# A pairwise bilinear product with operands laid out by the host and its result held transposed

## The chip, the cores and the metric

The kernel runs on one core of a Trainium2 chip. The metric is the device time of one execution in microseconds (us). TensorE does matrix products, VectorE the elementwise work out of PSUM, ScalarE copies, GpSimd and SyncE issue DMA transfers; 16 DMA engines move data between HBM and the core's SBUF. A PSUM bank holds 512 f32 values in each of 128 partitions, and there are eight banks. Work that the host does before and after the launch (transposing arrays) is not in the metric.

## The reference, cut to what matters

```python
# r_inputs: (1024, 32, 128) f32     batch b, field, d
# L0_rec_W: (496, 128, 128) f32     pair p, e, d
pairs = list(itertools.combinations(range(32), 2))   # (i, j) with i < j, by rising i
v_i = inputs[:, I_IDX, :]
v_j = inputs[:, J_IDX, :]
transformed = jnp.einsum('bpd,ped->bpe', v_i, W)
return transformed * v_j                             # (1024, 496, 128) f32
```

For each of the 496 pairs (i, j) of the 32 fields, field i of every batch row is multiplied by the pair's own 128 x 128 matrix, and the result elementwise by field j. The inputs have 16.8 MB (x) and 32.5 MB (w), the output has 260 MB.

## The kernel before, in words

Batch lies on the partitions: the 1024 rows are eight tiles of 128. `_chunks` cuts the pairs, in the reference's order, into 46 runs of at most 16 pairs with the same i and neighbouring j. The main loop (L122) goes over the chunks, and in each over the batch tiles. One product (L162, or L140 for chunks of at most four pairs) has a 128 x 128 block of x_i, transposed, as the stationary operand and up to four transposed matrices w_p side by side (512 columns) as the moving one. Two of them fill a PSUM tile `po` of two banks, of which there are three. VectorE multiplies the tile by the fields j of the batch tile (L169, L149), which lie side by side in `x_sb`, into an output tile `ot` (four buffers of 8 KB a partition), and SyncE stores it to HBM (L175). One row of such a store is n x 512 bytes long, where n is the number of pairs in the chunk.

TensorE needs the contracted dimension d on the partitions, but x and w come with batch and e there. So the kernel transposes both on TensorE, against an identity: each w_p (`transpose_w`, L86) and each 128 x 128 block of x_i (`transpose_x`, L93), into PSUM tiles `pt` (two), from which ScalarE copies them to SBUF (L87 into `wt`, L94 into `xt`). That is 496 transposes of w and 31 x 8 = 248 of x. `prepare(c + 1)` (L111) does this for the next chunk when the current one is halfway through its batch tiles, and issues the load of the chunk after that (L76). All loads are issued from GpSimd's queue. At the start come the first chunk's w, the fields 0 to 16 of x by batch tile (L103), the second chunk's w, and then the other fields (L106). x stays in SBUF for the whole run.

The order on each engine is that in which the program issues the instructions; waits between engines and for free buffers are put in by the tile framework.

Of the kernel before, what the change touches and what calls it, by code (L numbers as in the profile page):

```python
# [7 lines left out]

F32 = mybir.dt.float32
ALU = mybir.AluOpType  # L10

P = 128
BANK = 4  # 128-wide fp32 blocks in one PSUM bank
MAXC = 16  # pairs per chunk
MAXB = 8  # batch tiles


def _chunks(nf):
    """Runs of pairs (i, j0..j0+n-1) that share i; pair numbers run on in this order."""
    out = []  # L20
    p0 = 0
    for i in range(nf - 1):
        j0 = i + 1
        left = nf - 1 - i
        while left:
            if left > MAXC:
                n = min(MAXC, -(-left // (2 * BANK)) * BANK)
            else:
                n = left
            out.append((i, j0, p0, n))  # L30
            j0 += n
            p0 += n
            left -= n
    return out


@with_exitstack
def kernel(
    ctx: ExitStack,
    tc: tile.TileContext,  # L40
    x: bass.AP,
    w: bass.AP,
    out: bass.AP,
):
    """out[b, p, e] = (sum_d x[b, i(p), d] * w[p, e, d]) * x[b, j(p), e]

    Batch lies on partitions. For one i, the pairs (i, j) with j = i+1.. are
    contiguous in w, in out and, as fields j, in x, so one product of
    x_i^T (stationary) with up to four w_p^T side by side fills a PSUM bank,
    and its elementwise factor is a contiguous slice of x.  # L50
    """
    nc = tc.nc
    B, NF, D = x.shape
    NB = B // P
    assert NB == MAXB and D == P

    cpool = ctx.enter_context(tc.tile_pool(name="const", bufs=1))
    wpool = ctx.enter_context(tc.tile_pool(name="w", bufs=2))
    tpool = ctx.enter_context(tc.tile_pool(name="t", bufs=2))
    opool = ctx.enter_context(tc.tile_pool(name="o", bufs=4))  # L60
    ps_t = ctx.enter_context(tc.tile_pool(name="ps_t", bufs=2, space=bass.MemoryType.PSUM))
    ps_o = ctx.enter_context(tc.tile_pool(name="ps_o", bufs=3, space=bass.MemoryType.PSUM))

    ident = cpool.tile([P, P], F32, tag="ident", name="ident")
    make_identity(nc, ident)
    x_sb = cpool.tile([P, NB, NF, D], F32, tag="x", name="x_sb")

    x_v = x.rearrange("(b p) f d -> p b f d", p=P)
    out_v = out.rearrange("(b p) q e -> p b q e", p=P)

    chunks = _chunks(NF)

    def load_w(c):
        _, _, p0, n = chunks[c]
        t = wpool.tile([P, MAXC, D], F32, tag="wn", name=f"wn_{c}")
        nc.gpsimd.dma_start(out=t[:, :n, :], in_=w[p0 : p0 + n].rearrange("q e d -> e q d"))  # L76
        return t

    def transpose_w(c, wn):
        n = chunks[c][3]  # L80
        wt = tpool.tile([P, MAXC, D], F32, tag="wt", name=f"wt_{c}")
        for k in range(0, n, BANK):
            m = min(BANK, n - k)
            pt = ps_t.tile([P, BANK, P], F32, tag="pt", name=f"ptw_{c}_{k}")
            for r in range(m):
                nc.tensor.transpose(pt[:, r, :], wn[:, k + r, :], ident)  # L86
            nc.scalar.copy(wt[:, k : k + m, :], pt[:, :m, :])  # L87
        return wt

    def transpose_x(i, xt, b0, nb):  # L90
        pt = ps_t.tile([P, BANK, P], F32, tag="pt", name=f"ptx_{i}_{b0}")
        for r in range(nb):
            nc.tensor.transpose(pt[:, r, :], x_sb[:, b0 + r, i, :], ident)  # L93
        nc.scalar.copy(xt[:, b0 : b0 + nb, :], pt[:, :nb, :])  # L94

    def new_xt(i):
        return tpool.tile([P, NB, P], F32, tag="xt", name=f"xt_{i}")

    # The first chunk needs x only up to its last field: those come first.
    w_nat = {0: load_w(0)}  # L100
    f0 = chunks[0][1] + chunks[0][3]
    for b in range(NB):
        nc.gpsimd.dma_start(out=x_sb[:, b, :f0, :], in_=x_v[:, b, :f0, :])  # L103
    w_nat[1] = load_w(1)
    for b in range(NB):
        nc.gpsimd.dma_start(out=x_sb[:, b, f0:, :], in_=x_v[:, b, f0:, :])  # L106

    w_t = {0: transpose_w(0, w_nat.pop(0))}
    x_t = {0: new_xt(0)}

    def prepare(c):  # L111
        """Transposed operands of chunk c, made while chunk c-1 is at work."""
        if c + 1 < len(chunks):
            w_nat[c + 1] = load_w(c + 1)
        w_t[c] = transpose_w(c, w_nat.pop(c))
        i = chunks[c][0]
        if i not in x_t:
            x_t[i] = new_xt(i)
            for b0 in range(0, NB, BANK):
                transpose_x(i, x_t[i], b0, BANK)  # L120

    for c, (i, j0, p0, n) in enumerate(chunks):  # L122
        wt, xt = w_t.pop(c), x_t[i]
        # batch tiles per store, and per PSUM tile (two banks)
        nb = 1
        while nb * 2 * n <= MAXC and nb < NB:
            nb *= 2
        bpb = BANK // n if n <= BANK else 0
        for b0 in range(0, NB, nb):
            ot = opool.tile([P, MAXC * D], F32, tag="ot", name=f"ot_{c}_{b0}")  # L130
            o4 = ot[:, : nb * n * D].rearrange("p (b q e) -> p b q e", b=nb, q=n)
            if c == 0:
                for b in range(b0, b0 + nb):
                    transpose_x(i, xt, b, 1)
            if bpb:
                for s in range(0, nb, 2 * bpb):
                    po = ps_o.tile([P, 2, BANK * D], F32, tag="po", name=f"po_{c}_{b0}_{s}")
                    for k in range(2):
                        for r in range(bpb):
                            nc.tensor.matmul(  # L140
                                po[:, k, r * n * D : (r + 1) * n * D],
                                xt[:, b0 + s + k * bpb + r, :],
                                wt[:, :n, :],
                                start=True,
                                stop=True,
                            )
                    for k in range(2):
                        bo = s + k * bpb
                        nc.vector.tensor_tensor(  # L149
                            o4[:, bo : bo + bpb],  # L150
                            po[:, k, : bpb * n * D].rearrange("p (b q e) -> p b q e", b=bpb, q=n),
                            x_sb[:, b0 + bo : b0 + bo + bpb, j0 : j0 + n, :],
                            ALU.mult,
                        )
            else:
                for r in range(nb):
                    for k in range(0, n, 2 * BANK):
                        m = min(2 * BANK, n - k)
                        po = ps_o.tile([P, 2 * BANK, D], F32, tag="po", name=f"po_{c}_{b0}_{r}_{k}")
                        for h in range(0, m, BANK):  # L160
                            g = min(BANK, m - h)
                            nc.tensor.matmul(  # L162
                                po[:, h : h + g, :],
                                xt[:, b0 + r, :],
                                wt[:, k + h : k + h + g, :],
                                start=True,
                                stop=True,
                            )
                        nc.vector.tensor_tensor(  # L169
                            o4[:, r, k : k + m, :],  # L170
                            po[:, :m, :],
                            x_sb[:, b0 + r, j0 + k : j0 + k + m, :],
                            ALU.mult,
                        )
            nc.sync.dma_start(out=out_v[:, b0 : b0 + nb, p0 : p0 + n, :], in_=o4)  # L175
            half = (NB // 2) // nb * nb
            if b0 == half and c + 1 < len(chunks):
                prepare(c + 1)


_INS = ["r_inputs", "L0_rec_W"]
_OUT = ((1024, 496, 128), "float32")


# [17 lines left out]
```

## Time and profile before

| What | Value |
|---|---|
| Median of 3 runs | 979.3 us (979.02 to 979.58) |
| Profiled execution: span of its instructions (the page gives no other time for it) | 975.6 us |
| TensorE, products and transposes | busy 944.4 us, 97% |
| Weight loads (beside TensorE's products) | busy 483.9 us, 50% |
| VectorE | busy 611.5 us, 63% |
| ScalarE | busy 105.5 us, 11% |
| GpSimd | busy 55.8 us, 6% |
| HBM | read 49.28 MB, written 260.05 MB |
| DMA queue of SyncE (stores) | 65.9% of 16 engines' span |
| DMA queue of GpSimd (loads) | 16.0% of 16 engines' span |

The profile is that of one execution. Its lines name engines as PE (TensorE products), PEld (TensorE weight loads), DVE (VectorE), ACT (ScalarE), POOL (GpSimd) and SP (SyncE), and the source line after an L. A group of instructions is given with its count, its busy time, the mean ns of one, the idle time of the engine ahead of them and what ended it. A product of f32 operands stands in the counts as two passes. The ends of products are modelled, so that neighbouring ones overlap; their starts are measured.

### The profile page before, as it was taken

The page shows a single profiled execution, that of the slowest core. Times are in us where ns is not written, and L with a number is a line of the kernel's source. Part 1 is how long each engine was busy: PE and PEld are TensorE (multiplying, and loading weights), DVE is VectorE, ACT ScalarE, POOL GpSimd, SP SyncE. Part 2 cuts the span into 40 slices and gives each one's busy share as a digit, 9 for nine tenths or more (in the row PEclk, how much of TensorE's full clock was granted, in tenths as well). Part 3 has the DMA queues.
Part 4 walks back from the last instruction along what each step waited for, and adds up shares of the span by engine and source line. Part 5 has one row for each costly group of instructions (what it writes and reads, how often), then busy time and mean ns, then how long its engine had stood idle before and what let it go on. Part 6 is the DMA issues. An engine that isn't in the chain of part 4 may idle for free.

```text
span 975.6 us, 7916 instructions
## 1 busy us (share of the span) xinstructions
PE 944.4 (97%) x2920; PEld 483.9 (50%) x2920; DVE 611.5 (63%) x630; ACT 105.5 (11%) x205; POOL 55.8 (6%) x68
## 2 busy tenths in 40 slices
PE   6598999999999999999999999999999999999997
PEld 3244454544445454544545554455544555555565
DVE  2264666666666666666666666666666666666664
ACT  1101010000101010110101011011110011110111
POOL 3100000000000000000000000000000000000000
PEclk9798999999999999999999999999999999999999
DMA  8999777878787878787888878888887877777876
GB/s 334 424 422 368 306 311 324 326 299 342 296 339 303 327 294 339 308 320 297 328 321 310 319 307 300 327 314 320 339 295 317 313 312 303 305 296 283 303 294 219
DMA packets 63079, 309.85 MB, mean 318 GB/s; under 512 B 5953, under 2 KB 9025, under 8 KB 53825
## 3 DMA queue, kind: packets, MB, share of 16 engines
q1 hardware_dynamic: 52064, 260.07, 65.9%
q0 software_dynamic: 10976, 49.29, 16.0%
q8 instruction: 23, 0.38, 0.2%
q14 instruction: 16, 0.12, 0.0%
HBM read 49.28 MB, written 260.05 MB: 317 GB/s over the span
## 4 chain that ended last, share of the span: by engine, by line
PE 91%; DMA 7%; ACT 0%; POOL 0%; issue 0%; DVE 0%; DVEq 0%; POOLq 0%; ACTq 0%
PE po L162 81%; DMA wn<-in_L_rec_W_dram 7%; PE ptw L86 6%; PE ptx L93 3%; PE po L140 2%; DMA x_sb<-in_r_inputs_dram 1%; ACT wt L87 0%; POOL wn L76 0%; DVE ot L149 0%; DVEq L198 0%; ACT xt L94 0%; POOL ident masks.py:199 0%; POOL ident masks.py:197 0%; POOLq masks.py:199 0%; ACTq L87 0%
## 5 line engine op out<-in xcount | busy, mean ns | idle before, releaser
L162 PE MATMUL po<-wt,xt 128*128 128x512 f32 (+3 forms) x2112 | 853.8, 559 | 2.3 <-ACT xt L94 2.3
L169 DVE TENSOR_TENSOR ot<-po,x_sb 128x1024 f32<-128x1024 f32 (+3 forms) x608 | 598.4, 1008 | 350.3 <-PE po L162 344.8
L162 PEld LDWEIGHTS po<-wt,xt 128*128 128x128 f32 x2112 | 386.0, 190 | 407.7 <-issue 346.6
L87 ACT COPY wt<-ptw 128x512 f32<-128x512 f32 (+3 forms) x136 | 69.5, 550 | 822.8 <-PE ptw L86 822.8
L76 POOL DMA_DIRECT2D wn<-in_L_rec_W_dram x46 | 46.6, 1014 | 870.2 <-PE ptw L86 787.0
L86 PE MATMUL ptw<-ident,wn 128*128 128x128 f32 x496 | 71.8, 286 | 22.7 <-DMA wn<-in_L_rec_W_dram 22.7
L86 PEld LDWEIGHTS ptw<-ident,wn 128*128 128x128 f32 x496 | 62.2, 148 | 55.6 <-issue 28.7
L94 ACT COPY xt<-ptx 128x512 f32<-128x512 f32 (+1 forms) x68 | 35.9, 550 | 39.5 <-PE ptx L93 39.0
L93 PEld LDWEIGHTS ptx<-ident,x_sb 128*128 128x128 f32 x248 | 29.0, 141 | 16.4 <-ACT wt L87 9.7
L93 PE MATMUL ptx<-ident,x_sb 128*128 128x128 f32 x248 | 36.5, 276 | 0.5 <-ACT wt L87 0.4
L149 DVE TENSOR_TENSOR ot<-po,x_sb 128x512 f32<-128x512 f32 (+1 forms) x22 | 13.1, 638 | 9.6 <-PE po L140 9.6
L140 PE MATMUL po<-wt,xt 128*128 128x512 f32 (+3 forms) x64 | 18.2, 438 | 0.1
L140 PEld LDWEIGHTS po<-wt,xt 128*128 128x128 f32 x64 | 10.7, 190 | 6.3 <-issue 3.1
L106 POOL DMA_DIRECT2D x_sb<-in_r_inputs_dram x8 | 4.3, 533 | 27.5 <-DMA x_sb<-in_r_inputs_dram 21.2
L103 POOL DMA_DIRECT2D x_sb<-in_r_inputs_dram x8 | 4.3, 554 | 1.8 <-DMA wn<-in_L_rec_W_dram 1.8
L87 ACT ACT_TABLE_LOAD x1 | 1.3, 1283 | 0.7 <-PEq L190 0.7
masks.py:199 POOL TENSOR_SCALAR_AFFINE_SELECT ident<-ident 128x128 f32<-128x128 f32 x1 | 0.3, 305 | 0.1
masks.py:197 POOL MEMSET ident<- 128x128 f32 x1 | 0.2, 204 | 0.3 <-POOLq L190 0.3
L190 POOL MEMSET const-float32-0.0<- 128x1 f32 x1 | 0.1, 98 | 0.2 <-issue 0.2
L190 POOL MEMSET const-bfloat16-1.0<- 128x1 bf16 x1 | 0.1, 101 | 0.0
L190 POOL MEMSET const-uint8-127<- 128x1 uint8 x1 | 0.1, 101 | 0.0
L190 POOL MEMSET const-float32-1.0<- 128x1 f32 x1 | 0.1, 98 | 0.0
## 6 DMA issues: line engine op xcount, KB each, us to landing
out_dram<-ot SPq DMA_DIRECT2D x75, 1024.0 KB, 4.0
out_dram<-ot SPq DMA_DIRECT2D x98, 768.0 KB, 3.4
out_dram<-ot SPq DMA_DIRECT2D x24, 896.0 KB, 3.7
out_dram<-ot SPq DMA_DIRECT2D x32, 640.0 KB, 3.0
out_dram<-ot SPq DMA_DIRECT2D x24, 704.0 KB, 3.3
out_dram<-ot SPq DMA_DIRECT2D x16, 960.0 KB, 4.0
out_dram<-ot SPq DMA_DIRECT2D x24, 576.0 KB, 3.0
out_dram<-ot SPq DMA_DIRECT2D x16, 832.0 KB, 3.4
```

What stands on the lines that cost most here:

```text
L76: nc.gpsimd.dma_start(out=t[:, :n, :], in_=w[p0 : p0 + n].rearrange("q e d -> e q d"))
L86: nc.tensor.transpose(pt[:, r, :], wn[:, k + r, :], ident)
L87: nc.scalar.copy(wt[:, k : k + m, :], pt[:, :m, :])
L93: nc.tensor.transpose(pt[:, r, :], x_sb[:, b0 + r, i, :], ident)
L94: nc.scalar.copy(xt[:, b0 : b0 + nb, :], pt[:, :nb, :])
L103: nc.gpsimd.dma_start(out=x_sb[:, b, :f0, :], in_=x_v[:, b, :f0, :])
L106: nc.gpsimd.dma_start(out=x_sb[:, b, f0:, :], in_=x_v[:, b, f0:, :])
L140: nc.tensor.matmul(po[:, k, r * n * D : (r + 1) * n * D], xt[:, b0 + s + k * bpb + r, :], wt[:, :n, :], start=True, stop=True,)
L149: nc.vector.tensor_tensor(o4[:, bo : bo + bpb], po[:, k, : bpb * n * D].rearrange("p (b q e) -> p b q e", b=bpb, q=n), x_sb[:, b0 + bo : b ...
L162: nc.tensor.matmul(po[:, h : h + g, :], xt[:, b0 + r, :], wt[:, k + h : k + h + g, :], start=True, stop=True,)
L169: nc.vector.tensor_tensor(o4[:, r, k : k + m, :], po[:, :m, :], x_sb[:, b0 + r, j0 + k : j0 + k + m, :], ALU.mult,)
L190: nc = _bacc.Bacc("TRN2", target_bir_lowering=False, num_devices=1)
```

## The change

The host now hands over x as `xt` of shape (d, field, batch) and w as `wt` of shape (d, pair, e), with the pairs sorted by rising j (and by rising i within one j). It takes the output as (pair, e, batch) and turns it back after the launch.

On the chip, each pair has two products: the stationary operand is the pair's w with d on the partitions and e as its columns, the moving operand is x_i with d on the partitions and 512 batch rows as its columns. The result has e on the partitions and batch on the free dimension and fills a PSUM tile of two banks (four such tiles). VectorE multiplies the 1024 columns by x_j in the same layout (d and e have the same size and partition, so that one copy of x serves as both operands). Two pairs share an output tile of 1 MB (six buffers), and SyncE stores it in rows of 4 KB; the last two pairs are multiplied and stored by halves.

There are no transposes, no copies on ScalarE and no identity. w is loaded in chunks of eight pairs (512 KB, four buffers), issued from ScalarE's queue three chunks ahead. Each field of x is a tile of its own (512 KB); the fields 0 to 3 are issued from SyncE at the start, the fields 4 and 5 from ScalarE, and field j + 3 from ScalarE at the first pair with j.

The diff, cut to its core:

```diff
-def _chunks(nf):
-    """Runs of pairs (i, j0..j0+n-1) that share i; pair numbers run on in this order."""
...
+def _pairs():
+    return [(i, j) for j in range(1, NF) for i in range(j)]
...
-    def transpose_w(c, wn):
...
-                nc.tensor.transpose(pt[:, r, :], wn[:, k + r, :], ident)
-            nc.scalar.copy(wt[:, k : k + m, :], pt[:, :m, :])
...
-    def transpose_x(i, xt, b0, nb):
...
-    def prepare(c):
...
+    xpool = ctx.enter_context(tc.tile_pool(name="x", bufs=1))
+    wpool = ctx.enter_context(tc.tile_pool(name="w", bufs=4))
+    opool = ctx.enter_context(tc.tile_pool(name="o", bufs=6))
+    ppool = ctx.enter_context(tc.tile_pool(name="ps", bufs=4, space=bass.MemoryType.PSUM))
+
+    def load_x(f, eng, pieces=1):
+        x_sb[f] = xpool.tile([P, BT], F32, tag=f"x{f}", name=f"x_{f}")
+        s = BT // pieces
+        for k in range(pieces):
+            eng.dma_start(out=x_sb[f][:, k * s : (k + 1) * s], in_=xt[:, f, k * s : (k + 1) * s])
+
+    def load_w(c, splits=(0, WC)):
+        w_sb[c] = wpool.tile([P, WC, P], F32, tag="w", name=f"w_{c}")
+        for a, b in zip(splits, splits[1:]):
+            nc.scalar.dma_start(out=w_sb[c][:, a:b, :], in_=wt[:, c * WC + a : c * WC + b, :])
+
+    load_w(0, (0, 1, 3, WC))
+    load_x(0, nc.sync, 2)
+    load_x(1, nc.sync, 2)
+    load_x(2, nc.sync)
+    load_w(1)
+    load_x(3, nc.sync)
+    load_w(2)
+    load_x(4, nc.scalar)
+    load_x(5, nc.scalar)
+
+    out_v = out.rearrange("q e b -> e q b")
+    for q, (i, j) in enumerate(pairs):
+        if q % WC == 0 and q // WC + 3 < nchunk:
+            load_w(q // WC + 3)
+        if i == 0 and 5 < j + 3 < NF:
+            load_x(j + 3, nc.scalar)
+        po = ppool.tile([P, BT], F32, tag="po", name=f"po_{q}")
+        for h in range(0, BT, HB):
+            nc.tensor.matmul(
+                po[:, h : h + HB],
+                w_sb[q // WC][:, q % WC, :],
+                x_sb[i][:, h : h + HB],
+                start=True,
+                stop=True,
+            )
+        r = q % OC
+        if r == 0:
+            ot = opool.tile([P, OC, BT], F32, tag="ot", name=f"ot_{q}")
+        if q < NQ - OC:
+            nc.vector.tensor_tensor(ot[:, r, :], po[:, :], x_sb[j][:, :], ALU.mult)
+            if r == OC - 1:
+                nc.sync.dma_start(out=out_v[:, q - r : q + 1, :], in_=ot[:, :, :])
+        else:
+            for h in range(0, BT, HB):
+                s = slice(h, h + HB)
+                nc.vector.tensor_tensor(ot[:, r, s], po[:, s], x_sb[j][:, s], ALU.mult)
+                nc.sync.dma_start(out=out_v[:, q, s], in_=ot[:, r, s])
...
+    perm = _np.array([i * (2 * NF - 1 - i) // 2 + j - i - 1 for i, j in _pairs()])
+    xt = _np.ascontiguousarray(x.transpose(2, 1, 0))
+    wt = _np.ascontiguousarray(w[perm].transpose(2, 0, 1))
...
+    args.append(nc.dram_tensor("out_0_dram", (NQ, P, BT), F32, kind="ExternalOutput").ap())
...
+    y[:, perm, :] = got.transpose(2, 0, 1)
```

Here P = 128, NF = 32, NQ = 496, BT = 1024, HB = 512, WC = 8 and OC = 2.

More of the change, by code (lines that the diff above doesn't have):

```diff
@@ L5 @@
 from concourse import mybir
-from concourse.masks import make_identity
 from concourse._compat import with_exitstack
@@ L12 @@
 P = 128
-BANK = 4
-MAXC = 16
-MAXB = 8
-def _chunks(nf):
[L20 to L34, printed above, removed]
+NF = 32
+NQ = NF * (NF - 1) // 2
+BT = 1024
+HB = 512
+WC = 8
+OC = 2
+def _pairs():
+    return [(i, j) for j in range(1, NF) for i in range(j)]
 @with_exitstack
@@ L40 @@
     tc: tile.TileContext,
-    x: bass.AP,
-    w: bass.AP,
+    xt: bass.AP,
+    wt: bass.AP,
     out: bass.AP,
@@ L52 @@
     nc = tc.nc
[L53 to L77, printed above, removed]
@@ L79, in transpose_w @@
-    def transpose_w(c, wn):
[L80 to L88, printed above, removed]
-    def transpose_x(i, xt, b0, nb):
[L91 to L109, printed above, removed]
-    def prepare(c):
[L113 to L178, printed above, removed]
@@ L181 @@
-_INS = ["r_inputs", "L0_rec_W"]
-_OUT = ((1024, 496, 128), "float32")
+    pairs = _pairs()
+    xpool = ctx.enter_context(tc.tile_pool(name="x", bufs=1))
+    wpool = ctx.enter_context(tc.tile_pool(name="w", bufs=4))
+    opool = ctx.enter_context(tc.tile_pool(name="o", bufs=6))
+    ppool = ctx.enter_context(tc.tile_pool(name="ps", bufs=4, space=bass.MemoryType.PSUM))
+    x_sb = {}
+    def load_x(f, eng, pieces=1):
[3 more added lines that the diff above has]
+            eng.dma_start(out=x_sb[f][:, k * s : (k + 1) * s], in_=xt[:, f, k * s : (k + 1) * s])
@@ new lines @@
+    nchunk = NQ // WC
+    w_sb = {}
+    def load_w(c, splits=(0, WC)):
[11 more added lines that the diff above has]
+    load_x(5, nc.scalar)
@@ new lines @@
+    out_v = out.rearrange("q e b -> e q b")
+    ot = None
+    for q, (i, j) in enumerate(pairs):
[24 more added lines that the diff above has]
+                nc.sync.dma_start(out=out_v[:, q, s], in_=ot[:, r, s])
```

11 lines of the change are left out of this document (6 added, 5 removed).

## The prediction

> **What bounds the kernel now.** I read the page first: spans, busy times, slices, the chain that ended last and the costliest groups.
>
> ```profile
> span 975.6 us, 7916 instructions
> PE 944.4 (97%) x2920; PEld 483.9 (50%) x2920; DVE 611.5 (63%) x630; ACT 105.5 (11%) x205; POOL 55.8 (6%) x68
> ...
> HBM read 49.28 MB, written 260.05 MB: 317 GB/s over the span
> ...
> PE po L162 81%; DMA wn<-in_L_rec_W_dram 7%; PE ptw L86 6%; PE ptx L93 3%; PE po L140 2%; DMA x_sb<-in_r_inputs_dram 1%; ACT wt L87 0%; POOL wn L76 0%; DVE ot L149 0%; DVEq L198 0%; ACT xt L94 0%; POOL ident masks.py:199 0%; POOL ident masks.py:197 0%; POOLq masks.py:199 0%; ACTq L87 0%
> ```
>
> The reader is to see that TensorE is busy in 97% of the span and that the chain runs through its own work: the products (L162, L140), the transposes of w (L86) and of x (L93), and near the start through loads. VectorE is far from the bound. Memory traffic is 309.3 MB, and its rate comes next, from the view of windows (columns: TensorE, weight loads, VectorE, ScalarE, GpSimd busy, the granted clock, the DMA engines' busy share, GB/s).
>
> ```profile
> 0.00:24.00 24.00, 14.49 (x42) 7.74 (x43) 5.71 (x5) 4.33 (x8) 9.60 (x20) 1.00 0.87 332
> 24.00:48.00 24.00, 12.98 (x39) 6.57 (x38) 6.54 (x6) 3.22 (x8) 2.82 (x5) 0.79 1.01 424
> 48.00:73.00 25.00, 24.64 (x61) 11.22 (x60) 16.57 (x14) 0.27 (x1) 1.56 (x2) 1.00 1.01 422
> 73.00:98.00 25.00, 20.63 (x64) 11.31 (x63) 10.84 (x10) 3.39 (x6) 1.15 (x1) 0.86 0.96 371
> ...
> 400.00:600.00 200.00, 200.00 (x590) 98.82 (x589) 132.46 (x151) 18.00 (x34) 8.96 (x9) 1.00 0.81 314
> ...
> 910.00:922.70 12.70, 12.70 (x38) 6.33 (x37) 8.98 (x8) 1.30 (x4) 0.00 (x0) 1.00 0.86 318
> 948.00:955.00 7.00, 7.00 (x21) 3.26 (x20) 4.82 (x8) 0.00 (x0) 0.00 (x0) 1.00 0.52 199
> ...
> 950.00:976.00 26.00, 19.69 (x89) 12.90 (x88) 12.71 (x22) 4.58 (x9) 0.55 (x1) 0.98 0.63 224
> ```
>
> There are two regimes. Up to about 75 us the DMA engines are full (share 1.01, 424 GB/s) and TensorE has gaps. After 98 us TensorE has none (200.00 of 200.00 us) and the DMA engines follow at 0.81. So the main part is worth exactly what TensorE no longer has to do, as long as the DMA engines can follow the faster pace.
>
> **What one pair costs.** VectorE takes up each finished 1024-column PSUM tile as soon as it is there; in the timeline of a stretch without transposes (chunk i=15, 16 pairs) the starts therefore show TensorE's step.
>
> ```profile
> 709.62 1.22 DVE L169 TENSOR_TENSOR ot<-po,x_sb 128x1024 f32<-128x1024 f32 x1 [0.89 <-PE po L162]
> ...
> 725.07 1.22 DVE L169 TENSOR_TENSOR ot<-po,x_sb 128x1024 f32<-128x1024 f32 x1 [0.49 <-PE po L162]
> ```
>
> Nine steps lie between these two: (725.07 - 709.62) / 9 = 1.717 us for 1024 columns. That is two products of 512 columns, each recorded as two passes, so 0.429 us a pass. In the kernel before, 496 pairs times 8 batch tiles times 128 columns are 507,904 columns, or 496 such tiles. The changed kernel has 496 pairs times 1024 batch columns: the same 496 tiles. 496 x 1.717 = 851.6 us, before and after. Turning the product round (w stationary, x moving) changes no size: both operands stay 128 x 128 and 128 x 512 f32, and the weights are loaded once a pass in both.
>
> ```profile
> L162 PEld LDWEIGHTS po<-wt,xt 128*128 128x128 f32 x2112 | 386.0, 190 | 407.7 <-issue 346.6 <-DVE ot L169 40.4 <-ACT xt L94 5.6
> L169 DVE TENSOR_TENSOR ot<-po,x_sb 128x1024 f32<-128x1024 f32 x352 | 431.1, 1225 | 312.5 <-PE po L162 309.8 <-DMA out_dram<-ot 2.7
> ```
>
> A weight load of 190 ns lies beside a pass of 429 ns and stays hidden; uncovered, 1,984 of them would cost 377 us, but nothing in the change removes the cover. VectorE's multiply of 1024 columns keeps its form (PSUM and SBUF operand, both contiguous): 1.225 us against TensorE's 1.717 us, 496 x 1.225 = 608 us in all. It stays hidden, with 0.49 us to spare a pair, and four PSUM tiles of two banks instead of three let TensorE run a tile further ahead.
>
> **What is removed.** All 496 + 248 transposes, their copies on ScalarE, and the identity. The price of a warm transpose is read where a group of eight stands between two products in TensorE's timeline (the starts count, since the ends are modelled and overlap).
>
> ```profile
> 703.50 1.02 PE L162 MATMUL po<-wt,xt 128*128 128x512 f32 x2
> 704.36 1.04 PE L86 MATMUL ptw<-ident,wn 128*128 128x128 f32 x8
> 705.23 0.39 PE L162 MATMUL po<-wt,xt 128*128 128x128 f32 x2
> ```
>
> 705.23 - 704.36 = 0.87 us for eight, 0.109 us each; 744 x 0.109 = 81 us, all on the path. ScalarE's copies are off it and give nothing by themselves, but for those of the first chunk. The waits of TensorE, the start and the end:
>
> ```profile
> PE ptw L86 <- DMA wn<-in_L_rec_W_dram: 22.7, 3, 10.1
> PE po L162 <- ACT xt L94: 2.3, 6, 0.5
> ...
> 8.27 3.73 PE L86 MATMUL ptw<-ident,wn 128*128 128x128 f32 x16 [8.27 <-DMA wn<-in_L_rec_W_dram]
> ...
> 970.10 1.29 DVE L149 TENSOR_TENSOR ot<-po,x_sb 128x512 f32<-128x512 f32 x2 [2.04 <-PE po L140]
> ```
>
> The 22.7 us include the first 8.3 us; the idle time behind it stands in the windows, 25.3 us short of full up to 98 us (9.5 + 11.0 + 0.4 + 4.4). Account of before: 851.6 + 81 + 25.3 + 5.5 (from 970.1 to 975.6) = 963.4. The 12 us left are the stretches at a lower clock after waits and the first chunk, where single transposes, their copies and products alternate; they have no cause in the new kernel except at its start.
>
> **What is added.** *Start.* SyncE and ScalarE issue the loads at once, in the order of need. The first product needs 64 KB of w and 256 KB of x. Rows:
>
> ```profile
> out_dram<-ot SPq DMA_DIRECT2D x1, 512.0 KB, 3.2
> ...
> wn<-in_L_rec_W_dram POOLq DMA_DIRECT2D x1, 64.0 KB, 2.2
> ...
> SPq L190 <- PEq L190: 0.7, 1, 0.7
> ...
> L175 SPq DMA_DIRECT2D out_dram<-ot x310: 332/332/388, 17.8 to 971.4; - x155
> ```
>
> The queue is free at 0.7 us, an issue takes 0.33 us, and 256 KB that share the engines with the w pieces land in about 3 us, between the rows of 2.2 and 3.2: 4.0 us. Bounds: 3.0 (0.7 + 2.2) and the 8.3 us of before. *Cold clock.* After the wait that ends at 79.3 us the chain of waits shows two passes in twice the warm time:
>
> ```profile
> 81.29 1.71 PE po L162 x2
> ```
>
> 0.855 us a pass instead of 0.429. From 79.3 us, cold transposes and these passes fill some 4 us, so the new kernel, which begins cold, loses about half of 4 us: 2.0 (bounds 0 and 4, if an early wait makes it cold again). *Inputs in the first stage.* Pairs run by rising j, so field j is needed only at pair j(j-1)/2, and each load of a field is issued three j ahead. ScalarE's queue holds these loads behind those of w: the load of chunk c+3 waits until TensorE has ended chunk c-1, and a field's load may stand behind it. Field 8, the first so held, is issued when pair 7 has ended and needed at pair 28, some 35 us later, while the slowest loads below took 33.2 us with the engines full and sixteen of them (16.8 MB) queued:
>
> ```profile
> DMA to landing us min/median/max: 7.9/28.3/33.2
> ```
>
> I cost it at nothing. The load of w three chunks ahead has 24 pairs (41 us) of cover. If that cover goes, TensorE waits and VectorE and the stores behind it. *Stores.* SyncE's queue holds four fields' loads and then only stores of 1 MB, each waiting for VectorE's second multiply; nothing else is behind them. Their rows are 4 KB everywhere, where before they ran from 8 KB down to 0.5 KB with the width of the chunk. The worst moment is the sixteenth pair, near 5.8 + 16 x 1.717 = 33 us: 16 x 0.524 = 8.4 MB stored, five w chunks 2.6 MB, ten fields 5.2 MB, 16.2 MB in all, where 424 GB/s moves 13.7 MB in 32 us. The 2.5 MB that it is behind fit in the five 1 MB output tiles beside the one being filled. Cost nothing; below 340 GB/s it would stall VectorE. Later the need is 0.59 MB per 1.717 us, or 343 GB/s, and 309.3 MB / 859 us = 360 GB/s on average. What the DMA engines can do is the unknown that counts: full, they moved 424; in the other windows the rate at a full share is 314/0.81 = 388, 318/0.86 = 370, 199/0.52 = 383 and at the very end, with rows of 0.5 to 1.5 KB, 224/0.63 = 356. For rows of 4 KB I take 380 to 424, nearest to the 388 and 424 of wide chunks, so it is hidden. *End.* The last pair is multiplied and stored in halves: 0.65 us, an issue of 0.33 and a landing of about 3, with little queued ahead: 4.5 us, against 5.5 before (bounds 3.5 and 6).
>
> **The sum.** 4.0 + 2.0 + 851.6 + 4.5 = 862.1 us of span. The page gives a span and no separate time for the profiled execution; the median of the runs, 979.3, is 3.7 us above it, which I keep: 865.8, said as 865.5.
>
> **A rule weighed against the trace.** The windows show 424 GB/s for 24 us and 422 for 25. The Trainium skill, "DMA: Bandwidth & Descriptors", section "Where 436 GB/s comes from", says that for transfers between HBM and SBUF the HBM side binds at about 358 GB/s per core. By it the time would be an estimate of 309.3 / 0.358 = 864 us of transfers alone, about 875 in all. The trace goes against it in those windows; the skill's "HBM Reference", section "Specifications (TRN2)", itself allows about 425 for a core that streams alone.
>
> **The rivals.** *DMA engines become the bound.* The windows with 424 are full of reads of x; where stores dominate, no window shows more than 318, since nothing asked for more. If 4 KB stores run at the worst ratio, 356 GB/s, 309.3 MB take 869 us, with 1 us ahead and some 4 us behind, 874 of span, 878 in all. VectorE would wait for output tiles and TensorE for PSUM all along. Against it: 383 with rows of 2 KB (948 to 955 us). The skill's rule above, as a rival, is this one; its 875 lies at the same place. *The start slips.* A load of x or w comes late in the first 60 us as w did before: three waits of up to 10.1 us, 22.7 in all. One such wait with a cold restart, 10 + 2, gives 877; the small issue order above speaks against it. *Slower than before.* The stores collapse: one pair is now one contiguous 512 KB block, where the DMA engines had written rows far apart; if this order brings the mixed rate under 309.3 / 975 = 317 GB/s, the kernel is slower; at 300 GB/s it takes 1031 + 9 = 1040 us. For it, only that no row here shows that order; against it, that no row with busy engines converts to under 356. *The change doesn't do what it says*, because transposes were hidden beside something else: no, since TensorE had 200.00 of 200.00 us.
>
> **How the numbers follow.** Forecast 0.74; DMA bound 0.13; slip at the start 0.09; stores collapse 0.04. A measurement of this kernel tells some 0.2% (2 us) from no change; only the last case comes near, shared as 0.03 slower and 0.01 same. The forecast's own range is 860 to 870 (start, cold clock and end at their bounds). Eight in ten reaches over most of the DMA case and the slip: 860 to 879. There TensorE's 851.6 us + 3.7 and the least start and end are a floor near 860.
>
> **What would show it.** Right: TensorE's first product near 4 us; VectorE starts 1.717 us apart from 10 us to the end; DMA share 0.85 to 0.95 in the middle, above 0.95 only in the first 60 us; no L86 or L93; VectorE waiting on TensorE alone. Wrong: VectorE waiting for output tiles (the store), a share near 1.0 through the middle, TensorE's step above 1.717, or gaps with a granted clock under 1.00 after 10 us.

## The result and the profile after

| | before | after |
|---|---|---|
| Median device time | 979.2 us | 878.4 us (877.9 to 878.9) |
| Ratio to before, 95% interval | | 0.8982 (0.8959 to 0.9005) |
| Profiled run: time, span | span 975.6 us | 878.0 us, span 876.1 us |

The kernel takes 10% less time (by the two medians of this job the ratio is 0.8971, inside the interval). That is 13 us more than the 865.5 us forecast. The measured time stands at the upper edge of the range of 860 to 879, and by the ratio to the median shown then (0.8982 x 979.3 = 879.6) just outside it. The page of the changed kernel, cut to the lines that answer to those of before:

```profile
span 876.1 us, 5490 instructions
PE 856.6 (98%) x1984; PEld 377.1 (43%) x1984; DVE 606.3 (69%) x498; POOL 0.2 (0%) x4
...
DMA  9999999989898898998988889888898989889877
GB/s 349 421 419 421 421 420 415 357 340 354 333 352 342 338 357 333 349 339 341 353 340 346 339 346 352 339 345 339 351 343 341 346 338 355 342 338 351 329 311 296
...
HBM read 49.28 MB, written 260.05 MB: 353 GB/s over the span
...
PE 88%; DMA 11%; DVE 0%; ACTq 0%; DVEq 0%; issue 0%; SPq 0%
...
L82 PE MATMUL po<-x,w 128*128 128x512 f32 x1984 | 856.6, 594 | 13.9 <-DVE ot L93 9.9
L93 DVE TENSOR_TENSOR ot<-po,x 128x1024 f32<-128x1024 f32 x494 | 603.7, 1225 | 264.7 <-PE po L82 228.1
```

The transposes are gone and 1,984 passes are left. What does not fit the forecast is in the last three lines: 11% of the chain is DMA, and TensorE waited 9.9 us for VectorE to give PSUM tiles back. The row of GB/s shows where: the second to the seventh slice (22 to 153 us) run at 415 to 421, the full rate, and only then does the traffic fall to some 330 to 357, around the 343 that the products ask for. The view of waits says what VectorE itself waited for, and the windows give the stage (columns as in the prediction, without ScalarE, which has no computing instruction left).

```profile
DVE ot L93 <- PE po L82: 228.1, 458, 2.7
DVE ot L93 <- DMA out_dram<-ot: 25.3, 12, 3.8
PEld po L82 <- DVE ot L93: 18.1, 12, 2.1
DVE ot L93 <- DMA x<-in_xt_dram: 11.2, 4, 9.2
PE po L82 <- DVE ot L93: 9.9, 9, 1.3
```

```profile
40.00:50.00 10.00, 10.00 (x25) 4.47 (x24) 6.67 (x6) 0.00 (x0) 1.00 1.03 419
50.00:60.00 10.00, 9.22 (x23) 3.84 (x22) 4.64 (x4) 0.00 (x0) 1.00 1.03 420
60.00:80.00 20.00, 15.30 (x35) 6.01 (x34) 9.49 (x9) 0.00 (x0) 1.00 1.03 421
80.00:100.00 20.00, 15.57 (x36) 6.04 (x35) 9.97 (x9) 0.00 (x0) 1.00 1.03 420
100.00:150.00 50.00, 50.00 (x118) 22.21 (x117) 37.39 (x32) 0.00 (x0) 1.00 1.02 418
200.00:300.00 100.00, 100.00 (x235) 44.27 (x234) 71.51 (x59) 0.00 (x0) 1.00 0.90 347
```

From 50 to 100 us TensorE has gaps while the DMA engines are full; at 200 us it has none. In VectorE's timeline the stall has sharp edges:

```profile
44.52 1.23 DVE L93 TENSOR_TENSOR ot<-po,x 128x1024 f32<-128x1024 f32 x1 [0.49 <-PE po L82]
46.78 2.40 DVE L93 TENSOR_TENSOR ot<-po,x 128x1024 f32<-128x1024 f32 x2 [1.03 <-DMA out_dram<-ot]
52.93 2.36 DVE L93 TENSOR_TENSOR ot<-po,x 128x1024 f32<-128x1024 f32 x2 [3.75 <-DMA out_dram<-ot]
...
113.49 1.23 DVE L93 TENSOR_TENSOR ot<-po,x 128x1024 f32<-128x1024 f32 x1 [0.45 <-PE po L82]
```

Between the first and the last of these lie 33 pairs in 68.97 us, where 33 x 1.717 = 56.7 us were needed: 12.3 us lost, to output tiles whose store had not landed. Why the stores were late shows in ScalarE's queue, which issues the loads of w (L61) and of the fields of x (L53):

```profile
10.06 0.34 ACTq L61 DMA_DIRECT2D w<-in_wt_dram  x1
10.44 12.57 ACTq L53 DMA_DIRECT2D x<-in_xt_dram  x5
23.11 0.43 ACTq L61 DMA_DIRECT2D w<-in_wt_dram  x1
23.57 18.44 ACTq L53 DMA_DIRECT2D x<-in_xt_dram  x8
42.11 0.44 ACTq L61 DMA_DIRECT2D w<-in_wt_dram  x1
46.68 16.10 ACTq L53 DMA_DIRECT2D x<-in_xt_dram  x8
64.22 0.33 ACTq L61 DMA_DIRECT2D w<-in_wt_dram  x1
67.22 12.52 ACTq L53 DMA_DIRECT2D x<-in_xt_dram  x5
```

The program issues one field at the first pair of each j. In the queue five, eight, eight and five fields follow one load of w: all 32 fields have been issued by 80 us, while TensorE is near pair 39, where j = 9 and the program would have asked for 13. So the tile framework put the instructions of this queue in an order of its own. How it chooses is not shown here; what can be seen is that the loads it moved ahead wait for no buffer, and that the loads of w which they passed wait for the end of a chunk. (The sentence in the section on the kernel before, that each engine keeps the order of the program, is wrong for this kernel.) An estimate of the cost: nineteen fields too early are 10 MB, 24 us of the full DMA engines at 420 GB/s; the five output tiles beside the one being filled can hold back 5.2 MB, 12.5 us. The rest, some 11 us, is near the 12.3 us lost.

### The profile page after: what moved, and what is told of

The parts are those of the page before. It is cut to its first block, busy times and chain, and to the rows that moved or that the text cites. A ratio compares the mean times of both kernels' runs of the same rounds, so it can differ in the third digit from the quotient of the medians.

```text
span 876.1 us, 5490 instructions
## 1 busy us (share of the span) xinstructions
PE 856.6 (98%) x1984; PEld 377.1 (43%) x1984; DVE 606.3 (69%) x498; POOL 0.2 (0%) x4
## 4 chain that ended last, share of the span: by engine, by line
PE 88%; DMA 11%; DVE 0%; ACTq 0%; DVEq 0%; issue 0%; SPq 0%
PE po L82 88%; DMA x<-in_xt_dram 6%; DMA out_dram<-ot 3%; DMA w<-in_wt_dram 2%; DVE ot L93 0%; DVE ot L99 0%; DVEq L121 0%; ACTq L61 0%; ACTq L53 0%; DVEq L93 0%; SPq L95 0%
## 5 line engine op out<-in xcount | busy, mean ns | idle before, releaser
L82 PE MATMUL po<-x,w 128*128 128x512 f32 x1984 | 856.6, 594 | 13.9 <-DVE ot L93 9.9
L93 DVE TENSOR_TENSOR ot<-po,x 128x1024 f32<-128x1024 f32 x494 | 603.7, 1225 | 264.7 <-PE po L82 228.1
L82 PEld LDWEIGHTS po<-x,w 128*128 128x128 f32 x1984 | 377.1, 190 | 492.6 <-issue 470.0
L99 DVE TENSOR_TENSOR ot<-po,x 128x512 f32<-128x512 f32 x4 | 2.6, 687 | 0.9 <-PE po L82 0.9
```

Of the source, the lines that this page charges most:

```text
L82: nc.tensor.matmul(po[:, h : h + HB], w_sb[q // WC][:, q % WC, :], x_sb[i][:, h : h + HB], start=True, stop=True,)
L93: nc.vector.tensor_tensor(ot[:, r, :], po[:, :], x_sb[j][:, :], ALU.mult)
L99: nc.vector.tensor_tensor(ot[:, r, s], po[:, s], x_sb[j][:, s], ALU.mult)
```

## The experiments

The theory to be tested, "early fields": the bytes of the fields come too early and take the DMA engines from the stores. Its rivals: "stores too slow" (4 KB rows cannot keep up, whatever comes beside them), and "shared counters". The last one comes from another view, what SyncE's queue waited for in the changed kernel:

```profile
SPq L95 <- DVE ot L93: 685.0, 234, 5.6
SPq L95 <- DMA x<-in_xt_dram: 67.8, 17, 7.2
```

Seventeen stores waited 67.8 us in all for the landing of a field's load that they have nothing to do with. The view does not say why. The reading taken here is that the loads of ScalarE's queue and the stores share a few semaphores (the counters that report a landing), and that an instruction that takes one up again waits for its last user. The stall might be those late issues, not the bytes. The median of before differed between the later jobs (976.1 and 977.3 us, runs from 972.9 to 979.5), so that kernels are compared with each other by their own times and spans; ratios are to the runs of before in the same job.

**The queue kept in the order of the program.**

```diff
-            eng.dma_start(out=x_sb[f][:, k * s : (k + 1) * s], in_=xt[:, f, k * s : (k + 1) * s])
+            tc.keep_in_program_order(
+                eng.dma_start(out=x_sb[f][:, k * s : (k + 1) * s], in_=xt[:, f, k * s : (k + 1) * s])
+            )
```

The loads of w are kept in the same way.

> The loads on ScalarE's queue are kept in the order in which the program issues them, so that field j + 3 is loaded near the time of pair j and not ahead of the waiting loads of w. Theory 'early fields' (all 28 fields on ScalarE's queue land in the first 85 us, some 9 MB earlier than needed; their bytes take the DMA engines from the stores, the output tiles run out, and VectorE loses 12.3 us between 45 and 113 us): the stall goes, 878.4 - 12.3 = 866 us, between 865 and 868, and VectorE waits for the store less than 2 us in all. Rival 'stores too slow' (4 KB rows do not move fast enough in the first 100 us whatever comes beside them): 875 to 879. Rival 'shared counters' (stores are issued late because they wait for the landing of a load that shares their semaphore): about 866 as well; the next run tells it apart.

Measured: 865.3 us, ratio 0.8867 (0.8844 to 0.8891), span 864.2 us. In ScalarE's queue the loads of w and of the fields now alternate (an extract of four comes first below), and no wait of VectorE for a store is left; its two longest waits are:

```profile
34.62 0.33 ACTq L64 DMA_DIRECT2D w<-in_wt_dram  x1
34.99 0.88 ACTq L54 DMA_DIRECT2D x<-in_xt_dram  x1
48.35 0.33 ACTq L64 DMA_DIRECT2D w<-in_wt_dram  x1
48.72 1.05 ACTq L54 DMA_DIRECT2D x<-in_xt_dram  x1
```

```profile
DVE ot L97 <- PE po L86: 239.7, 488, 0.5
DVE ot L97 <- DMA x<-in_xt_dram: 11.4, 3, 9.3
```

```profile
50.00:100.00 50.00, 50.00 (x118) 22.10 (x117) 35.69 (x30) 0.00 (x0) 1.00 1.02 397
```

TensorE is busy in 50.00 of 50.00 us where it had 40, with stores and loads moving at 397 GB/s. "Stores too slow" falls: the same stores keep up once the fields are spread out. The stores issued between 20 and 100 us now take a median of 8.7 us to land, where they took 14.2 in the changed kernel. "Shared counters" predicts the same time here.

**The fields from 6 on from GpSimd's queue**, whose landings are counted apart from those of the stores.

```diff
-            load_x(j + 3, nc.scalar)
+            load_x(j + 3, nc.gpsimd)
```

> The fields from 6 on are loaded from GpSimd's queue, which has semaphores of its own; they still run ahead with no pacing. Theory 'early fields': the same bytes come as early or earlier, the stall stays or grows: 877 to 884 us, VectorE waiting for the store by 20 us or more in all. Rival 'shared counters': no store waits for the landing of one of these fields any more, so the stall goes: 866 to 869 us.

Measured: 881.3 us, ratio 0.9034 (0.9010 to 0.9058), span 881.1 us.

```profile
DVE ot L93 <- DMA out_dram<-ot: 25.5, 9, 3.7
```

```profile
SPq L95 <- DMA x<-in_xt_dram: 3.6, 1, 3.6
```

```profile
1.23 4.31 POOL L53 DMA_DIRECT2D x<-in_xt_dram  x8 [0.79 <-POOLq L115]
POOL x L53 <- DMA x<-in_xt_dram: 46.3, 18, 3.4
```

The stores' wait for fields fell from 67.8 to 3.6 us, and the stall did not go: VectorE waits for stores as long as in the changed kernel (25.5 against 25.3 us). "Shared counters" falls as its cause. Against the paced kernel the span is 16.9 us longer, where the changed kernel's is 11.9; VectorE's wait for fields, which lies at the start, grew from 11.2 to 16.3 us. "No pacing" was not quite so: GpSimd issues eight of these loads at once, and each of the other eighteen only when an earlier load has landed. All 26 are still issued by 61.4 us, and the stores issued between 20 and 100 us take a median of 20.1 us to land.

**Seven output tiles instead of six.**

```diff
-    opool = ctx.enter_context(tc.tile_pool(name="o", bufs=6))
+    opool = ctx.enter_context(tc.tile_pool(name="o", bufs=7))
```

> Seven output tiles instead of six, nothing else. Theory 'early fields': one more tile holds 1.05 MB more of the stores that are behind, worth 1.05 MB / 0.42 GB/ms = 2.5 us: 876 us. Rival 'shared counters': the store's issue is late and not its room, but a further tile also lets VectorE go on by two pairs, up to 3.4 us less. Rival 'stores too slow' for the whole run: no change, 878.4.

Measured: 874.8 us, ratio 0.8964 (0.8940 to 0.8987), span 872.9 us. That is 3.2 us less than the changed kernel by the profiled spans and 3.6 us by the medians, over the 2.5 us of the room alone and about the 3.4 us of two pairs. It shows that room for late stores counts, against "stores too slow for the whole run"; between "early fields" and "shared counters" it does not decide.

**744 transposes put back on TensorE**, six behind every fourth pair.

```diff
...
+        if q % 4 == 0:
+            pt = [tpool.tile([P, 4, P], F32, tag="pt", name=f"pt_{q}_{k}") for k in range(2)]
+            for k in range(6):
+                nc.tensor.transpose(pt[k // 3][:, k % 3, :], w_sb[q // WC][:, q % WC + k % 4, :], ident)
```

> 744 transposes of w blocks against an identity are put back on TensorE, six behind every fourth pair; nothing reads them, ScalarE copies nothing, and three PSUM tiles are left for the products. The prediction's price of 0.109 us each on the path: +81 us. Theory 'early fields': since the slower pace needs 314 instead of 343 GB/s, some 2.6 MB instead of 5.1 MB are beyond the room at 90 us, so 6 us of the stall go: 878.4 + 81 - 6 = 953 us. If the stall does not depend on the pace: 959. If transposes among products are hidden in part: less than 945.

Measured: 955.1 us, ratio 0.9789 (0.9763 to 0.9814), against 953 expected; nearly the whole gain is gone. The price reads from the steady stretch:

```profile
200.00:800.00 600.00, 600.00 (x1757) 291.08 (x1756) 390.77 (x320) 0.00 (x0) 1.00 0.82 314
```

A pair has 4 passes and 1.5 transposes, so 1,757 records are 319.5 pairs, 1.878 us each; (1.878 - 1.717) / 1.5 = 0.107 us a transpose, 80 us for 744. The prediction had 0.109. The span of 952.8 us leaves 952.8 - 864.2 - 80 = 8.6 us for the stall, less than the 11.9 of the changed kernel, as the slower pace should have it, but more than the 6 that was expected.

**The pairs by rising i**, with the queue in order.

```diff
-    return [(i, j) for j in range(1, NF) for i in range(j)]
+    return [(i, j) for i in range(NF) for j in range(i + 1, NF)]
```

> The paced kernel with the pairs by rising i (the reference's order) instead of rising j, so that all 32 fields are needed within the first 31 pairs. Theory 'early fields': by pair 31 some 36.8 MB are asked for (16.3 stored, 16.8 of x, 3.7 of w) where 420 GB/s moves 23.9 MB; 12.9 MB behind, 3.8 MB of room, 9.1 MB / 0.42 = 22 us of stall: 865.3 + 22 = 887 us, with VectorE waiting both for fields and for the store. Rival (the stall was an effect of the queue's hoisting and not of bytes): 865 to 868, since the order on ScalarE's queue is kept here too.

Measured: 890.8 us, ratio 0.9123 (0.9094 to 0.9152), expected 887. The wait has moved from the store to the fields:

```profile
DVE ot L97 <- DMA x<-in_xt_dram: 49.5, 25, 9.7
```

The expectation had VectorE wait for the store as well, and no such wait is there: the size came out, the place of the wait did not. The stall needs no reordered queue; many bytes asked for at the start are enough, though here they hold up the fields and not the stores. The rising j is worth 25 us (890.8 against 865.3), but only if the queue keeps it; the changed kernel had half of that.

**Operands from the host alone**: the tiling and the output of the kernel before, w and x transposed by the host.

```diff
-        nc.gpsimd.dma_start(out=t[:, :n, :], in_=w[p0 : p0 + n].rearrange("q e d -> e q d"))
+        nc.gpsimd.dma_start(out=t[:, :n, :], in_=w[:, p0 : p0 + n, :])
...
+    def load_xt(i):
+        t = tpool.tile([P, NB, P], F32, tag="xt", name=f"xt_{i}")
+        nc.gpsimd.dma_start(out=t, in_=xt_d[:, i, :].rearrange("d (b p) -> d b p", p=P))
+        return t
```

> The tiling of the kernel before (batch on partitions, output as in the reference, chunks by rising i, loads from GpSimd), but the transposed w and x come from the host and are loaded; x is loaded twice, as it is and transposed. No transposes on TensorE, no copies on ScalarE, four PSUM tiles. This is the one part 'operands from the host' without 'result held transposed' and 'rising j'. Theory: the steady part is the same as in the changed kernel (1.717 us a 1024-column tile), so the 81 us of transposes go; the early burst of x stays: by pair 31 some 13.8 MB behind, 2.1 MB of room, 28 us; with a start near 9 us 893 to 897 us. If the layout of the result gave something of its own in the steady part, TensorE's step or its waits would be larger than 1.717 us there, and the time above 900. If the early burst did not matter: about 870.

Measured: 905.8 us, ratio 0.9277 (0.9252 to 0.9302), outside the 893 to 897 expected and above the 900 that stood for a slower steady part. But the excess is at the start and not in the steady part, as TensorE's waits, a late window and the end of the chain show:

```profile
PE po L135 <- DMA xt<-in_xt_dram: 24.9, 2, 17.1
```

```profile
200.00:400.00 200.00, 200.00 (x491) 91.79 (x490) 142.73 (x143) 6.81 (x13) 1.00 0.91 355
```

```profile
95.14 784.57 PE po L135 x1984
879.71 17.28 PE po L113 x64
```

The transposed field of the second i stands on GpSimd's queue behind the sixteen loads of x; it is issued at 59.6 us and takes 35.4 us to land, and TensorE waits 17.1 us for it and starts cold again (slow passes from 95.1 to 100.2 us). From then on TensorE works without a gap, 801.9 us for the 465 pairs left, whose work is 465 x 1.717 = 798.4 us. So the layout of the result changes nothing in the steady part. The steps by the ratios: this kernel is 0.072 below before, the changed kernel a further 0.030 lower (transposed result, rising j and finer loads together), and the queue's order gives 0.012. These are differences of kernels, not prices of single parts: this one also loads x twice, which makes its start heavier.

**The paced kernel with TensorE warmed up.**

```diff
...
+    nc.vector.memset(zt[:, :], 0.0)
+    pw = ppool.tile([P, BT], F32, tag="po", name="pw")
+    for _ in range(7):
+        nc.tensor.matmul(pw[:, :HB], zt[:, :P], zt[:, :], start=True, stop=True)
```

> The paced kernel with seven short bf16 products of zeros on TensorE while the first loads are under way, whose result nobody reads. Theory: the paced kernel's TensorE needs 854.6 us for 851.6 us of work, the 3 us being passes at half speed at the start; with the clock up when the first product starts, 862 to 863 us. If the lower clock at the start does not come from the idle time ahead: 865.3.

Measured: 864.5 us (864.4 to 864.6), ratio 0.8854 (0.8831 to 0.8877), span 862.6 us, where 862 to 863 was expected. Of the kernels that do all the work it is the fastest, but by little. The profiled spans differ by 1.6 us from the paced kernel's, the medians by 0.8, and two of the paced kernel's four runs (864.62 and 864.71) are as fast to within 0.3 us; what the warming is worth stays open. What the trace does show is that work ahead of the first product brings the full clock sooner, so that the idle time is behind the slow passes, and that the seven products, from 1.18 us on, were too few to remove them all. Weight loads show the passes, 0.86 us apart while cold and 0.43 after; the first line is the last cold one of the warmed kernel, the second its first at full speed:

```profile
5.92 0.34 PEld L93 LDWEIGHTS po<-x,w 128*128 128x128 f32 x1 [0.52 <-issue]
6.68 0.19 PEld L93 LDWEIGHTS po<-x,w 128*128 128x128 f32 x1 [0.42 <-issue]
```

Without the warming (in the paced kernel) the same change comes between 9.28 and 9.96 us. The first load at full speed comes 5.5 us after TensorE's first work in the warmed kernel (1.18 to 6.68), 6.0 in the paced one (4.00 to 9.96) and 5.2 in the changed one (3.95 to 9.12).

**The DMA engines by themselves.**

```diff
...
-            nc.vector.tensor_tensor(ot[:, r, :], po[:, :], x_sb[j][:, :], ALU.mult)
+            nc.vector.tensor_tensor(ot[:, r, :], x_sb[i][:, :], x_sb[j][:, :], ALU.mult)
...
```

> The products are left out but for one per chunk of w that nobody reads; VectorE multiplies x_i by x_j out of SBUF. Loads, pacing by chunk, stores and their 4 KB rows are as in the paced kernel, so that VectorE (some 1.2 us a pair, 600 us in all) is faster than the DMA engines and these set the time. If 4 KB rows move at the rate of the early windows, 420 GB/s: 309.7 MB / 420 = 737 + 7 = 744 us. The prediction's lower bound, 356 GB/s: 877 us. Between: the rate follows from the time.

Measured: 763.8 us, expected 744. The DMA engines are full from 10 us on, but at two rates:

```profile
20.00:100.00 80.00, 34.22 (x34) 8.52 (x34) 42.99 (x37) 0.00 (x0) 0.54 1.03 421
500.00:700.00 200.00, 0.00 (x0) 0.00 (x0) 181.69 (x155) 0.00 (x0) 0.50 1.02 404
```

TensorE, with one product a chunk left, no longer held back the loads of w: they were all done within 300 us, ahead of the stores. While loads and stores are mixed, 421 GB/s; with stores alone, 404; the 744 us had supposed 420 throughout. Both rates are above the 343 GB/s that the changed kernel needs when steady, so that the DMA engines are no bound there.

## Why the prediction was right or wrong

**Right: the steady part.** One pair takes 1.717 us as before. In the changed kernel TensorE has no gap from 97.73 us to its end (first line, 450 pairs), and the paced kernel does the 496 pairs in one piece (second line):

```profile
97.73 772.78 PE po L82 x1800
4.00 854.60 PE po L86 x1984
```

The second is 851.6 us and 3.0 us of cold passes. The price of a transpose was right (0.107 measured, 0.109 predicted), and the start too (3.95 us, predicted 4.0).

**Wrong: "Inputs in the first stage", "I cost it at nothing".** The step took the queue's order from the program: "ScalarE's queue holds these loads behind those of w". The framework had turned that round. The term that belongs there is 12.3 us. Of the signs named ahead, the DMA share of 0.89 to 0.90 in the middle came. But VectorE waited for output tiles, which was named as a sign of being wrong, and the share stayed above 0.95 up to 150 us, where only the first 60 were to show that. The check of the worst moment (2.5 MB behind, with room for five tiles) was built on ten fields by the sixteenth pair and on that being the worst; with the queue as it was, 19 fields too many had been issued by 80 us. With the queue as the prediction thought it, the paced kernel measured 865.3 us and 864.2 us of span, against 862.1 + 3.7 predicted. That 865.3 stands so near 865.5 is partly luck: the span was 2.1 us longer than predicted, and the time around it 1.7 us and not 3.7.

**The account of the profiled run.** 862.1 us of span predicted + 12.3 stall + 1.0 end (5.5 us from TensorE's end at 870.5, predicted 4.5) + 0.7 cold clock (TensorE's 866.6 us from 3.95 to 870.5, less 851.6 and 12.3, leave 2.7, predicted 2.0) = 876.1, the measured span. The end had been costed with one half still to multiply, 0.65 us (the terms named there add up to 4.0, of which 4.5 was made); the trace has both halves after TensorE's end:

```profile
870.54 1.29 DVE L99 TENSOR_TENSOR ot<-po,x 128x512 f32<-128x512 f32 x2 [0.43 <-PE po L82]
```

The time around the span was 1.9 us, not 3.7, since the 3.7 had been the distance of a span to another run's median.

**The rivals.** "DMA engines become the bound" gave 878 in all and came nearest, but by luck: it had the right symptom, VectorE waiting for output tiles, yet for 70 us and not all along, and its rate of 356 GB/s is refuted for these rows by 404 and 421. "The start slips" gave 877, also with another cause: one load late, TensorE waiting for an operand. Here the loads were early and the stores late. Its argument against, "the small issue order above", is the step that failed. No collapse of the stores was seen.

The 358 GB/s of the Trainium skill ("DMA: Bandwidth & Descriptors", section "Where 436 GB/s comes from") did not bind these runs on one core, which moved 404 to 421 GB/s when their DMA engines were full. The 425 that the Trainium skill gives for a core streaming alone ("HBM Reference", section "Specifications (TRN2)") is near the 421.

## What to carry to other kernels

A load that waits for nothing is free to move ahead of one that waits, when the queue's order is made by a scheduler; look at the queue's real order in the trace, or pin it, before costing a prefetch at nothing. Where a stage has full DMA engines, a load too early can cost time as one too late does (12 us here, 25 with the fields late): count the bytes that the queue will issue by each moment against the rate, and take the room of the output buffers from the difference. A transfer hidden in the average (353 GB/s of 420) can still decide the first 100 us.

## What was not expected of the hardware

Stores alone with 4 KB rows moved 404 GB/s with the DMA engines full, mixed with loads 421. TensorE's first full-speed weight load came 5.2 to 6.0 us after its first work in the changed kernel and the two paced ones, where the prediction had taken 4; the slow passes took 0.86 us instead of 0.43. Between 20 and 100 us, with the DMA engines full in all three, the median landing time of a 1 MB store went from 8.7 us (fields paced) to 14.2 (early on ScalarE's queue) and 20.1 (early on GpSimd's).
